# A selective scan rebuilt: broadcasts by DMA, decays in PSUM, products on GpSimd

## The chip, the core and the metric

The kernel runs on one core of a Trainium2 chip. Its time is the device time of one execution in microseconds (us). The engines are named as in the profile: PE is TensorE (matmul), PEld its weight loads, DVE is VectorE, ACT is ScalarE, POOL is GpSimd, SP is SyncE, which here only issues DMAs.

## What is computed

The input is four images of 64 x 64 tokens with 96 channels. Four layers follow each other: a two-dimensional selective scan block, a separable convolution, a linear attention block, and a spectral filter, the last two with a feed-forward block behind them. Only the first layer is changed. Its core, from the reference (b = 4 images, d = 192 channels, n = 16 states, L = 4096 tokens):

```python
def step(h, inp):
    u_t, dt_t, B_t, C_t = inp
    dA = jnp.exp(dt_t[..., None] * A)
    h = dA * h + (dt_t * u_t)[..., None] * B_t[:, None, :]
    y = jnp.sum(h * C_t[:, None, :], axis=-1)
    return (h, y)
...
x_hw = xc.reshape(B, D_INNER, L)
x_wh = jnp.transpose(xc, (0, 1, 3, 2)).reshape(B, D_INNER, L)
x_hwwh = jnp.stack([x_hw, x_wh], axis=0)
xs = jnp.concatenate([x_hwwh, jnp.flip(x_hwwh, axis=3)], axis=0)
...
yy = y[0] + wh_y + inv_y[0] + invwh_y
```

Each image is scanned four times: by rows and by columns, each forwards and backwards. delta, B and C are computed token by token, so the four scans of an image use the same values in different orders. A depends on channel and state. In front of the scan stand a group norm, an input projection, a 3x3 convolution over 192 channels and the projections to delta, B and C; behind it the addition of D u, a gate, an output projection and the residual.

## The kernel before

Arrays stand with channels on the partitions and tokens along them. `layer0` has four parts, written as generators or functions whose pieces a driver strings together. A tile framework inserts the semaphores; it orders the instructions of each engine by the order of the program and by when tiles come free. A tile pool with a tag and a number of buffers (`bufs`) makes the next tile of that tag wait until an older one is released.

`pre(b)` makes everything ahead of the scan, in 8 blocks of 512 tokens: loads (SP), normalisation (ACT), projections and the convolution (PE, `p_conv`), silu and softplus (ACT and DVE). It stores `sz`, `u`, `bc`, `delta` and `du` (delta times u) to DRAM, by DMAs that POOL issues. `post(b)` makes what follows the scan, also in 8 blocks.

The scan works on groups of 8 channels: 8 channels x 16 states fill the 128 partitions, channel by channel. There are 24 groups an image, 96 in all. `decay(b, g)` loads delta of 8 channels (`dl`, 8 rows), lets PE copy each row to 16 partitions (a matmul with the 0/1 matrix `sel`, into `pa`, L248) and ACT write exp(delta A) to `dA` in SBUF (L252), 512 tokens at a time. `scan_group` does the same for du (`pb`, L275); DVE multiplies it with `brep`, B replicated on the partitions, into `dB` (L279). ACT copies both arrays into order by columns (`dAT`, `dBT`, L281). DVE then does the two scans by rows over 4096 tokens (L286, L287), their sum (L290), the two by columns (L294, L295), their sum (L298), the sum of both orders through a transposing view (L299), and the product with `crep`, C replicated (L307). PE sums over the states with the matrix `red` (`py`, L312), ACT copies the sums to `ys` (L315), SP stores them (L317).

In the middle of each group, `beside()` emits pieces of `post` of the image before and of `pre` of the image after, and the next group's `decay`. The first image's `pre` stands alone at the start, the last image's `post` alone at the end of the layer; `layers123` follows.

Of the kernel before, what the change touches and what calls it, by code (L numbers as in the profile page):

```python
# [18 lines left out]
NB = 4  # images  # L19
HW = 64  # rows, and columns, of an image  # L20
L = HW * HW  # tokens of an image
C = 96  # channels
DI = 192  # inner channels of the scan, and hidden ones of the spectral filter
NS = 16  # states of a scanned channel
NG = DI // 8  # groups of 8 scanned channels: 8 channels x 16 states on the partitions
RK = 6
BLK = 512  # tokens of one matmul: 8 image rows
# [3 lines left out]
N1 = 64  # the transform over 4096 tokens is 64 x 64  # L31


def conv_taps():
    """The 3x3 taps (ky, kx), the middle one first: it alone reaches every output."""
    return [(1, 1)] + [(y, x) for y in range(3) for x in range(3) if (y, x) != (1, 1)]


def tap_window(ky, kx, r0):
    """Rows (of the block's, from r0) and columns of the output that a tap reaches."""  # L40
    dy, dx = ky - 1, kx - 1
    ra, rb = max(0, -dy - r0), min(RPB, HW - dy - r0)
    ca, cb = max(0, -dx), min(HW, HW - dx)
    return dy, dx, ra, rb, ca, cb


@with_exitstack
def layer0(ctx: ExitStack, tc: tile.TileContext, a: dict, x1):
    """Group norm, the 2D selective scan block, the residual; x1[b] = relu(x + block), as the
    next layer reads it."""  # L50
# [20 lines left out]
    sel = const("sel", [40, 128], a["sel"])  # L71
# [3 lines left out]
    # Each of the four scans adds D u.  # L75
# [6 lines left out]

    delta_s = dram("delta_s", [DI, L])
    du_s = dram("du_s", [DI, L])
    bc_s = dram("bc_s", [2 * NS, L])
    u_s = dram("u_s", [DI, L])
    sz_s = dram("sz_s", [DI, L])
    y_s = dram("y_s", [DI, L])

    def halves(t):  # L90
        return t.rearrange("(c p) l -> p c l", p=C)
# [3 lines left out]

    def k4(name, shape=(C, 2, BLK)):
        return wk.tile(list(shape), F32, tag="k4", name=name, bufs=4)

    def pre_psum(name, rows=C, cols=BLK):
        t = ps.tile([128, BLK], F32, tag="pre", name=name, bufs=2)  # L100
        return t[:rows, :cols]

    def pre(b):
        """Everything before the scan, in blocks of 8 image rows."""
# [9 lines left out]
        # A group's three channels: its mean, and the mean of variance + squared distance of means.  # L114
# [15 lines left out]
        for i in range(NBLK):  # L130
# [4 lines left out]
            xb = k2("xb", (C, RPB + 2, HW))  # L135
# [3 lines left out]
            xn = k2("xn", (C, RPB + 2, HW))  # L139
            nc.scalar.activation(  # L140
                xn[:, :n, :], xb[:, :n, :], AF.Identity, scale=gn[:, 0:1], bias=gn[:, 1:2]
            )
            xp = k4("xp", (C, 2, RPB + 2, HW))
            for c in range(2):
                for ra, rb in ((0, 5), (5, n)):
                    p = pre_psum("p_xp", C, (rb - ra) * HW)
                    nc.tensor.matmul(
                        p, lhsT=w_in[:, c * C : (c + 1) * C], rhs=xn[:, ra:rb, :],
# [3 lines left out]
            sz = k4("sz")  # L152
            for c in range(2):
# [3 lines left out]
                    rhs=xn[:, r0 - lo : r0 - lo + RPB, :], start=True, stop=True,  # L157
                )
                nc.scalar.activation(sz[:, c, :], p, AF.Silu)  # L159
            nc.gpsimd.dma_start(halves(sz_s[b])[:, :, cols], sz)  # L160
            yield
            u = k4("u")
# [16 lines left out]
            nc.gpsimd.dma_start(halves(u_s[b])[:, :, cols], u)  # L179
# [8 lines left out]
            nc.gpsimd.dma_start(bc_s[b][:, cols], xd[RK : RK + 2 * NS, :])  # L188
            for c in range(2):
# [3 lines left out]
                # softplus(v) = max(v, 0) + log(1 + e), e = exp(-|v|); with w = fl(1 + e), the  # L193
                # logarithm is log(w) - ((w - 1) - e).
# [12 lines left out]
                nc.gpsimd.dma_start(delta_s[b][rows, cols], r)  # L207
                du = k2("du")
                nc.vector.tensor_tensor(du, r, u[:, c, :], ALU.mult)
                nc.gpsimd.dma_start(du_s[b][rows, cols], du)  # L210
            yield

    def post(b):
        """D u, the gate, the output projection and the residual."""
        for i in range(NBLK):
            cols = slice(i * BLK, (i + 1) * BLK)
            y, u, sz = k4("y_in"), k4("u_in"), k4("sz_in")
# [620 lines left out]
```

## Time and profile before

| | us |
|---|---|
| median of two runs | 9806.71 (9795.03 to 9818.39) |
| span of the profiled execution | 9822.7 |
| first scan (L286) starts | 491.7 |
| last copy of sums (L315) ends | 7413.6 |
| DVE busy over the span | 6735.3 (69%) |
| PE busy | 6680.7 (68%) |
| ACT busy | 3202.3 (33%) |
| POOL busy | 159.9 (2%) |

The span is from the first to the last instruction of one execution; the median is over runs of the whole program, and no other time of the profiled execution is given. Between 491.7 and 7413.6 lies the scan stage: 6921.9 us for 96 groups, 72.1 a group. Before it is the first image's `pre`, after it the last `post` and the three later layers. A group of instructions in the profile is one line of the code on one engine; "busy" is the sum of its durations, "mean" that of one. What stands behind the second bar is the time in which its engine was idle just before it, and who ended that idle time.

### The profile page before, as it was taken

The numbers are of one execution on the slowest core, as the hardware profiler recorded it, in microseconds if no ns is written. First come the engines' busy times: TensorE is split into PE (matmuls) and PEld (weight loads), VectorE is DVE, ScalarE is ACT, GpSimd is POOL, SyncE is SP. The second block draws the span as 40 slices with busy tenths as digits, with TensorE's granted clock in tenths as the row PEclk, the third lists the DMA queues.
The fourth block names the chain that finished last, engine by engine and source line by source line (L and its number), as shares of the span: only waits on it lengthen the run. The fifth ranks groups of instructions, "written<-read, shape, count | busy, mean of one in ns | idle before, by whom it ended". The sixth has DMA issues, their size and how long they took to land.

```text
span 9822.7 us, 58304 instructions
## 1 busy us (share of the span) xinstructions
PE 6680.7 (68%) x22202; PEld 3031.3 (31%) x22202; DVE 6735.3 (69%) x3526; ACT 3202.3 (33%) x4081; POOL 159.9 (2%) x296
## 2 busy tenths in 40 slices
PE   6767777754567666555666665554445888989888
PEld 2222222211122222111222211111112766848576
DVE  1188888887888888788988879989993323132232
ACT  3333434342334444333444433333330111121111
POOL 0000000000000000000000000000000000000000
PEclk8855565555566666555656655555556867777776
DMA  1110000002100000210000021000002010100000
GB/s 44 43 25 16 15 13 15 14 20 52 30 15 16 19 17 17 52 39 12 16 18 16 22 44 33 13 6 6 6 5 71 4 36 1 33 7 14 26 1 26
DMA packets 94661, 216.09 MB, mean 22 GB/s; under 512 B 25274, under 2 KB 26958, under 8 KB 92494
## 3 DMA queue, kind: packets, MB, share of 16 engines
q1 hardware_dynamic: 75950, 153.62, 6.4%
q0 software_dynamic: 18432, 58.74, 2.1%
q8 instruction: 177, 2.90, 0.1%
q14 instruction: 102, 0.84, 0.0%
HBM read 134.67 MB, written 77.59 MB: 22 GB/s over the span
## 4 chain that ended last, share of the span: by engine, by line
DVE 42%; PE 39%; ACT 8%; issue 8%; DMA 2%; SPq 0%; POOL 0%; DVEq 0%; ACTq 0%; POOLq 0%
DVE dB L287 8%; DVE T L294 8%; DVE dBT L295 6%; PE pb L275 6%; DVE S L286 6%; PE p_conv L169 5%; DVE S L290 4%; ACT dBT L281 4%; PE pa L248 4%; PE py L312 3%; PE p_l L499 3%; DVE S L299 2%; PE p_dft L653 2%; PE p_h L639 2%; ACT dAT L281 2%
## 5 line engine op out<-in xcount | busy, mean ns | idle before, releaser
L275 PE MATMUL pb<-du_g,sel 8*128 8x512 f32 x1536 | 1309.9, 1022 | 1517.7 <-DVE dB L279 1517.7
L248 PE MATMUL pa<-dl,sel 8*128 8x512 f32 x1536 | 1359.6, 1030 | 879.2 <-ACT dA L252 784.7
L281 ACT COPY dAT<-dA 128x512 f32<-128x512 f32 x768 | 772.3, 1104 | 2020.5 <-DVE dBT L295 2014.5
L286 DVE TENSOR_TENSOR_SCAN S<-dA,dB 128x4096 f32<-128x4096 f32 x96 | 834.4, 8692 | 576.2 <-PE py L312 494.2
L169 PE MATMUL p_conv<-xp,conv_w 96*96 96x504 f32 (+3 forms) x2304 | 1204.7, 684 | 2.8 <-ACT sz L159 2.8
L275 PEld LDWEIGHTS pb<-du_g,sel 8*128 8x128 f32 x1536 | 447.7, 307 | 2317.7 <-DVE dB L279 1843.4
L248 PEld LDWEIGHTS pa<-dl,sel 8*128 8x128 f32 x1536 | 411.2, 296 | 1762.8 <-ACT dA L252 1082.3
L287 DVE TENSOR_TENSOR_SCAN dB<-dA,dB 128x4096 f32<-128x4096 f32 x96 | 833.9, 8686 | 5.6 <-DVE S L286 0.5
L294 DVE TENSOR_TENSOR_SCAN T<-dAT,dBT 128x4096 f32<-128x4096 f32 x96 | 833.4, 8681 | 0.0
L295 DVE TENSOR_TENSOR_SCAN dBT<-dAT,dBT 128x4096 f32<-128x4096 f32 x96 | 833.2, 8679 | 0.1
L281 ACT COPY dBT<-dB 128x512 f32<-128x512 f32 x768 | 771.8, 1094 | 130.9 <-DVE T L298 80.8
L252 ACT ACTIVATE dA<-pa,nega 128x512 f32<-128x512 f32 x768 | 513.8, 685 | 715.2 <-PE pa L248 671.4
L299 DVE TENSOR_TENSOR S<-S,T 128x4096 f32<-128x4096 f32 x96 | 716.2, 7460 | 1.1
L169 PEld LDWEIGHTS p_conv<-xp,conv_w 96*96 96x96 f32 x2304 | 423.0, 190 | 802.8 <-issue 779.2
L279 DVE TENSOR_TENSOR dB<-pb,brep 128x512 f32<-128x512 f32 x768 | 492.9, 679 | 251.5 <-PE pb L275 201.8
L312 PE MATMUL py<-S,red 128*32 128x512 f32 x1536 | 401.7, 955 | 201.2 <-DVE S L307 177.3
L307 DVE TENSOR_TENSOR S<-S,crep 128x1024 f32<-128x1024 f32 x384 | 445.8, 1220 | 1.9
L290 DVE TENSOR_TENSOR S<-S,dB 128x4096 f32<-128x4096 f32 x96 | 424.4, 4421 | 2.0
L298 DVE TENSOR_TENSOR T<-T,dBT 128x4096 f32<-128x4096 f32 x96 | 423.9, 4416 | 0.3
L201 DVE TENSOR_SCALAR w<-e 96x512 f32<-96x512 f32 x64 | 26.3, 411 | 391.1 <-ACT e L199 391.1
L499 PE MATMUL p_l<-x,taps 96*96 96x504 f32 (+3 forms) x576 | 249.8, 597 | 29.8 <-DMA x<-x 29.8
L376 DVE COPY o<-p_o 128x192 f32<-128x192 f32 x64 | 22.9, 357 | 318.4 <-ACT o L372 318.4
(183 smaller groups left out, 6638.2 us busy)
## 6 DMA issues: line engine op xcount, KB each, us to landing
tw<-in_dft SPq DMA_DIRECT2D x32, 512.0 KB
sz_s<-sz POOLq DMA_DIRECT2D x32, 384.0 KB, 3.4
u_s<-u POOLq DMA_DIRECT2D x32, 384.0 KB, 3.4
delta_s<-r POOLq DMA_DIRECT2D x64, 192.0 KB, 2.4
du_s<-du POOLq DMA_DIRECT2D x64, 192.0 KB, 2.4
dl<-delta_s SPq DMA_DIRECT2D x384, 32.0 KB
du_g<-du_s SPq DMA_DIRECT2D x384, 32.0 KB
y_s<-ys SPq DMA_DIRECT2D x768, 16.0 KB
```

Source lines behind the costliest of these rows:

```text
L169: nc.tensor.matmul(p[:, ra:rb, ca:cb], lhsT=conv_w[:, kc, ky * 3 + kx, oc * C : (oc + 1) * C], rhs=xp[:, kc, at + ra : at + rb, ca + dx : ...
L248: nc.tensor.matmul(pa, lhsT=sel[0:8, :], rhs=dl[:, (q % 2) * BLK : (q % 2 + 1) * BLK], start=True, stop=True,)
L275: nc.tensor.matmul(pb, lhsT=sel[32:40, :], rhs=du[32:40, (q % 2) * BLK : (q % 2 + 1) * BLK], start=True, stop=True,)
L281: nc.scalar.copy(dst.rearrange("p (w h) -> p w h", h=HW)[:, :, hs], src[:, cols].rearrange("p (h w) -> p w h", w=HW),)
L286: nc.vector.tensor_tensor_scan(S, dA, dB, 0.0, ALU.mult, ALU.add)
L287: nc.vector.tensor_tensor_scan(dB[:, ::-1], dA[:, ::-1], dB[:, ::-1], 0.0, ALU.mult, ALU.add)
L290: nc.vector.tensor_tensor(S, S, dB, ALU.add)
L294: nc.vector.tensor_tensor_scan(T, dAT, dBT, 0.0, ALU.mult, ALU.add)
L295: nc.vector.tensor_tensor_scan(dBT[:, ::-1], dAT[:, ::-1], dBT[:, ::-1], 0.0, ALU.mult, ALU.add)
L299: nc.vector.tensor_tensor(S.rearrange("p (h w) -> p h w", w=HW), S.rearrange("p (h w) -> p h w", w=HW), T.rearrange(by_col, h=HW), ALU.add,)
L312: nc.tensor.matmul(py[k : k + 32, :], lhsT=red, rhs=S[:, cols], start=True, stop=True)
L499: nc.tensor.matmul(p3[:, ra:rb, ca:cb], lhsT=taps[:, ky * 3 + kx, :], rhs=x3[:, r0 + dy + ra : r0 + dy + rb, ca + dx : cb + dx], start=(k ...
```

## The change

The scan now runs in phases: (image, group, order), 192 of them, with order 0 by rows and 1 by columns. The layout on the partitions is state by state (16 states x 8 channels). The tokens go in steps of `CH` = 1024, four a phase.

- `load` fetches delta and du of 8 channels by DMA straight to 128 partitions, each row of 4 KB read 16 times: 8 DMAs of 512 KB a phase. The matrix `sel` and its matmuls are gone.
- `inputs`: POOL multiplies du with the replicated B in place, for the next phase.
- `decay`: ACT writes exp(delta A) of 1024 tokens to PSUM (two buffers of two banks), once for the forward scan and once more for the backward one.
- `scan`: DVE does four forward scans of 1024, each started from the last column of the one before, and four backward ones in place. POOL adds the two directions and multiplies with the replicated C. PE, ACT and SP then sum, copy and store as before, for each order by itself.
- `turn`: transposes an array of up to 96 rows: load 4096 tokens a row, four copies on ACT through a transposing view, four stores. `pre` calls it for bc and for each half of delta and du, `post` for each half of the sums by columns. This replaces the copies of L281 and the add of L299.
- `replicas`: four DMAs of 2 MB an image replace the 16 of 256 KB. `beside()` calls it in the last phase of an image.
- Every DMA that POOL issued in `layer0` is now issued by SP. Buffers of `pre` and `post` change: `xp` has one, `u` two, `xn` is gone (in place), and `post` works by halves of the channels.
- `beside()` spreads the pieces of `post` and `pre` over the first 42 of an image's 48 phases.

The matrix `red` and the layout of `a_logs` follow the new order of the partitions. The diff, without `pre`'s and the later layers' small edits:

```diff
+CH = 1024
+NCH = L // CH
...
+    delta_s = [dram("delta_s", [DI, L]), dram("deltaT_s", [DI, L])]
+    du_s = [dram("du_s", [DI, L]), dram("duT_s", [DI, L])]
+    bc_s = [dram("bc_s", [2 * NS, L]), dram("bcT_s", [2 * NS, L])]
+    y_s = [dram("y_s", [DI, L]), dram("yT_s", [DI, L])]
+    y2_s = dram("y2_s", [DI, L])
...
+    def turn(src, dst):
+        n = src.shape[0]
+        t = wk.tile([C, L], F32, tag="turn", name="turn")
+        nc.sync.dma_start(t[:n, :], src)
+        for q in range(NCH):
+            o = wk.tile([C, CH], F32, tag="turned", name="turned")
+            w = CH // HW
+            nc.scalar.copy(
+                o[:n, :].rearrange("p (w h) -> p w h", h=HW),
+                t[:n, :].rearrange("p (h w) -> p w h", w=HW)[:, q * w : (q + 1) * w, :],
+            )
+            nc.sync.dma_start(dst[:, q * CH : (q + 1) * CH], o[:n, :])
...
     def pre(b):
...
+        turn(bc_s[0][b], bc_s[1][b])
+        yield
+        for c in range(2):
+            rows = slice(c * C, (c + 1) * C)
+            turn(delta_s[0][b][rows, :], delta_s[1][b][rows, :])
+            yield
+            turn(du_s[0][b][rows, :], du_s[1][b][rows, :])
+            yield
     def post(b):
+        for c in range(2):
+            rows = slice(c * C, (c + 1) * C)
+            turn(y_s[1][b][rows, :], y2_s[b][rows, :])
+            yield
...
+            for c in range(2):
+                rows = slice(c * C, (c + 1) * C)
+                y, y2, u = k2("y_in"), k2("y2_in"), k2("u_in")
+                nc.sync.dma_start(y, y_s[0][b][rows, cols])
+                nc.sync.dma_start(y2, y2_s[b][rows, cols])
+                nc.sync.dma_start(u, u_s[b][rows, cols])
+                nc.vector.scalar_tensor_tensor(y, u, d4[:, c : c + 1], y, ALU.mult, ALU.add)
+                sz = k2("sz_in")
+                nc.sync.dma_start(sz, sz_s[b][rows, cols])
+                nc.vector.tensor_tensor(y, y, y2, ALU.add)
+                nc.vector.tensor_tensor(y, y, sz, ALU.mult)
+                nc.tensor.matmul(p, lhsT=w_out[:, c, :], rhs=y, start=(c == 0), stop=(c == 1))
...
-    def decay(b, g):
...
-    def scan_group(b, g, dA, brep, crep, beside):
...
+    def load(b, g, o):
+        rows = slice(g * 8, (g + 1) * 8)
+        dl, du = [], []
+        for q in range(NCH):
+            for dst, src, n, tag, bufs in ((dl, delta_s, "dl", "dl", 5), (du, du_s, "B", "B", 6)):
+                t = big.tile([128, CH], F32, tag=tag, name=n, bufs=bufs)
+                nc.sync.dma_start(
+                    t, src[o][b][rows, chunk(q)].unsqueeze(0).broadcast_to([NS, 8, CH])
+                )
+                dst.append(t)
+        return dl, du
+    def inputs(b, g, o, du):
+        for q in range(NCH):
+            nc.gpsimd.tensor_tensor(du[q], du[q], reps[o, 0][:, chunk(q)], ALU.mult)
+    def decay(g, dl, q):
+        pa = ps.tile([128, CH], F32, tag="pa", name="pa", bufs=2)
+        nc.scalar.activation(pa, dl[q], AF.Exp, scale=nega[:, g : g + 1])
+        return pa
+    def scan(b, g, o, dl, B, beside):
+        rows = slice(g * 8, (g + 1) * 8)
+        S = []
+        for q in range(NCH):
+            pa = decay(g, dl, q)
+            s = big.tile([128, CH], F32, tag="S", name="S", bufs=6)
+            nc.vector.tensor_tensor_scan(
+                s, pa, B[q], S[-1][:, CH - 1 : CH] if S else 0.0, ALU.mult, ALU.add
+            )
+            S.append(s)
+        beside()
+        last = None
+        for q in reversed(range(NCH)):
+            pa = decay(g, dl, q)
+            nc.vector.tensor_tensor_scan(
+                B[q][:, ::-1], pa[:, ::-1], B[q][:, ::-1],
+                last[:, 0:1] if last is not None else 0.0, ALU.mult, ALU.add,
+            )
+            last = B[q]
+            nc.gpsimd.tensor_tensor(S[q], S[q], B[q], ALU.add)
+            nc.gpsimd.tensor_tensor(S[q], S[q], reps[o, 1][:, chunk(q)], ALU.mult)
+            if q % 2 == 1:
+                py = ps.tile([128, BLK], F32, tag="py", name="py")
+            for k in range(2):
+                at = 32 * (2 * (q % 2) + k)
+                nc.tensor.matmul(
+                    py[at : at + 32, :], lhsT=red, rhs=S[q][:, k * BLK : (k + 1) * BLK],
+                    start=True, stop=True,
+                )
+            if q % 2 == 0:
+                ys = wk.tile([128, BLK], F32, tag="ys", name="ys", bufs=2)
+                nc.scalar.copy(ys, py)
+                for j in range(4):
+                    i = 2 * q + j
+                    nc.sync.dma_start(
+                        y_s[o][b][rows, i * BLK : (i + 1) * BLK], ys[32 * j : 32 * j + 8, :]
+                    )
+    reps = {}
+    def replicas(b):
+        for o in range(2):
+            for k in range(2):
+                t = big.tile([128, L], F32, tag=f"rep{o}{k}", name=f"rep{o}{k}")
+                nc.sync.dma_start(
+                    t, bc_s[o][b][k * NS : (k + 1) * NS, :].unsqueeze(1).broadcast_to([NS, 8, L])
+                )
+                reps[o, k] = t
     for _ in pre(0):
         pass
+    phases = [(b, g, o) for b in range(NB) for g in range(NG) for o in range(2)]
+    replicas(0)
+    loaded = load(*phases[0])
+    inputs(*phases[0], loaded[1])
+    for n, (b, g, o) in enumerate(phases):
+        here = n % (2 * NG)
+        if here == 0:
+            aside = chain(post(b - 1) if b > 0 else (), pre(b + 1) if b + 1 < NB else ())
+            n_aside = (NBLK + 2 if b > 0 else 0) + (3 * NBLK + 6 if b + 1 < NB else 0)
+            done = 0
+        nxt = phases[n + 1] if n + 1 < len(phases) else None
+        ahead = []
+        def beside():
+            nonlocal done
+            if nxt is not None:
+                if nxt[0] != b:
+                    replicas(nxt[0])
+                ahead.append(load(*nxt))
+                inputs(*nxt, ahead[0][1])
+            while done < min(n_aside, n_aside * (here + 1) // (2 * NG - 6)):
+                next(aside)
+                done += 1
+        scan(b, g, o, *loaded, beside)
+        if ahead:
+            loaded = ahead[0]
```

## The prediction

> **What bounds the kernel now.** I read the windows first (where is the time), then the costliest groups, then the chain of waits, then the DMA part. Lines, engines and tiles are those of the kernel before.
>
> The windows give the scan stage by itself, from the first scan (491.7) to the last copy of sums (7413.6). Columns: length, then busy time (instructions) of PE, PEld, DVE, ACT, POOL, then clock, DMA share, GB/s:
>
> ```profile
> 491.70:7413.60 6921.90, 4243.39 (x6892) 1325.99 (x6890) 6002.20 (x2203) 2643.22 (x3130) 106.21 (x192) 0.57 0.08 20
> ```
>
> 70% of the span is this stage. DVE is busy 6002 of 6922 us, POOL 106, DMA at 8%. The groups say with what; the figure after the bar is the sum, then the mean in ns:
>
> ```profile
> L286 DVE TENSOR_TENSOR_SCAN S<-dA,dB 128x4096 f32<-128x4096 f32 x96 | 834.4, 8692 | 576.2 <-PE py L312 494.2
> ...
> L299 DVE TENSOR_TENSOR S<-S,T 128x4096 f32<-128x4096 f32 x96 | 716.2, 7460 | 1.1
> ...
> L279 DVE TENSOR_TENSOR dB<-pb,brep 128x512 f32<-128x512 f32 x768 | 492.9, 679 | 251.5 <-PE pb L275 201.8
> ...
> L307 DVE TENSOR_TENSOR S<-S,crep 128x1024 f32<-128x1024 f32 x384 | 445.8, 1220 | 1.9
> L290 DVE TENSOR_TENSOR S<-S,dB 128x4096 f32<-128x4096 f32 x96 | 424.4, 4421 | 2.0
> ```
>
> Per group of 8 channels (96 of them) DVE does four scans (8.69 each, 34.7), the transposing add 7.46, two plain adds 8.8, the B products 5.1, the C products 4.6: 60.8 us of a stage step of 6921.9/96 = 72.1. The rest are waits at both ends of a group (py, pb). The chain of waits agrees:
>
> ```profile
> DVE 42%; PE 39%; ACT 8%; issue 8%; DMA 2%; SPq 0%; POOL 0%; DVEq 0%; ACTq 0%; POOLq 0%
> ```
>
> So a group is DVE's 60.8 us plus about 11 of hand-over. The new loop runs 192 phases (a group in one order of the image); per phase the old stage costs 36.05 us.
>
> **What DVE loses.** All but the scans leave it. A scan of 4096 takes 8.69, a plain product 1.220 at 1024 and 4.421 at 4096: slope 1.042 ns an element, 0.15 fixed. A scan is so 2.08 ns an element plus 0.15: 2.29 for 1024 tokens. A phase has eight, 18.3 us; with the work of `pre` and `post` under 21. DVE ceases to be the bound.
>
> **What POOL gets.** Twelve products or sums of 128x1024 a phase: 4 with B, 4 sums of directions, 4 with C. No such row exists: POOL's only work on data is
>
> ```profile
> L627 POOL MEMSET ln_s<- 1x4096 f32 x4 | 14.0, 3507 | 53.5 <-PE p_att L588 53.5
> L556 POOL MEMSET lt<- 128x4 f32 x32 | 3.3, 106 | 1814.5 <-PE p_gram L559 1776.7 <-DVE s L475 32.9 <-PE p_tok L554 4.9
> ```
>
> 0.856 ns an element for one written stream, 0.10 fixed. A product has three streams. All overlapped: 0.98 us for 1024; one after another: 2.73; two of three overlapped: 1.85. I take the middle of the last two, 2.29 (an estimate): the memset is the only POOL row, and I see no reason that all its streams run at once. 12 x 2.29 = 27.5 us a phase, more than DVE's 18.3: POOL becomes the bound.
>
> The Trainium skill speaks against this move ("GPSIMD Engine Reference", section "Performance versus the Vector engine"): elementwise work with two inputs is about twice as slow there, 4497 ns for 2048 fp32 elements. By that price an operation would be 2.25 and the total about 90 us lower; no run here shows it yet.
>
> **What POOL and DVE take from each other.** They hardly ever worked together in this trace, so ends only: nothing, or full exclusion (rival C). I put down only DVE's instructions that, like POOL's, read two SBUF operands: four of `pre` per half block, three of `post`, 64 and 48 an image, three images of each in the stage, 336 x 0.68 (row L206) = 228 us, 1.2 a phase. The scans now read one operand from PSUM.
>
> A rule of the skill bears on this ("SBUF — State Buffer", section "Who interferes with whom"): a DVE instruction with at most one SBUF input does not contend with GpSimd, one with two does and blocks for a whole instruction. It would make the exclusion of rival C nil; no trace here tests it.
>
> **DMA.** Eight loads of 512 KB a phase replace two 32 KB loads in each pair of blocks: 4.19 MB. To it come, per image, with 3.1 MB for 192 channels: `pre` reads x twice (3.4) and writes four arrays and bc (13.1), the seven turns read and write delta, du, y and bc (19.9), `post` reads four arrays and x and writes x1 (15.7), the replicas take 8.4. That is 60.5 MB, 1.3 a phase, and with 0.13 for the sums 5.6 MB a phase in all. The nearest shape is the `tw` load, also 512 KB in 128 rows of 4 KB; a window with one of them alone and one with all engines full at the head of the later layers, and then two windows of the replica loads before the first scan:
>
> ```profile
> 7504.00:7508.00 4.00, 0.00 (x0) 0.00 (x0) 3.65 (x13) 0.56 (x2) 0.00 (x0) 0.50 1.04 250
> ...
> 7840.00:7844.00 4.00, 3.52 (x28) 2.61 (x24) 0.68 (x1) 0.60 (x1) 0.00 (x0) 1.00 0.42 131
> ```
>
> ```profile
> 472.00:476.00 4.00, 0.00 (x0) 0.00 (x0) 0.00 (x0) 0.75 (x1) 0.00 (x0) 0.50 1.13 131
> 476.00:480.00 4.00, 0.00 (x0) 0.00 (x0) 0.00 (x0) 0.00 (x0) 0.00 (x0) 0.50 0.90 118
> ```
>
> 131/0.42 = 312 GB/s for `tw`; 118/0.90 to 131/1.13, about 120 GB/s, where eight loads each fill 16 partitions from one source. The new loads have the `tw` target (128 partitions, 4 KB rows) but a source read 16 times. I take the 250 of the full window: 5.6 MB are 22 us a phase, under POOL's 27.5; the 120 is rival B. A turn's load of 1.5 MB goes ahead of the phase's loads, 6.3 us at 250; the 21 turns that fall into the stage are 132 us, 0.7 a phase, which I charge in full because only two spare B tiles are there to cover.
>
> **Waits added, and what stands behind them.** SP: the load of a B tile waits for POOL's sum that frees it (6 tiles, 4 in use); behind it stand the stores of sums and all transfers of `pre` and `post`, which leave POOL's queue (0.52 to 0.67 us each there) for SP's. A phase has 8 loads, 8 stores and about 4 others: 20 x 0.35 (SP's dl and y_in rows: 0.26 to 0.44) = 7 us, hidden under 27. ACT: an exponential waits for a PSUM tile that a scan frees; behind it the copies of sums and `pre`. Eight of 0.685 + 512 x 0.844 ns (slope from the xp copies, 422 at 320 and 368 at 256) = 1.12 are 8.9 us, with sums, turns and `pre` about 15: hidden. If a convolution holds ACT (up to 30 us in the waits of `u`), DVE has 9 us a phase to give before POOL starves. PE loses the 2669 us of L275 and L248 and stays hidden. POOL: a sum waits for the reverse scan; behind it the next phase's products. Were these last in its queue, two scans (4.6 us) a phase would be bare; since the first two of the next phase's B tiles are free, I cost that at nothing (rival D is its price).
>
> **Start, image borders, end.** A turn is its load 7, then four times a transposing copy (2.0, from L281's 1.10 for 512) and a store of 384 KB (3.4 to landing) through one buffer: 29 us. Three must be done before the first phase by columns, less the phase before it: 60; `pre` has fewer buffers (one xp for four): 5 us for each of 8 blocks, 40. Start 100. At three image borders 8.4 MB of replicas precede the loads: 8.4/0.25 = 34 us each, 101. (The C products of an image's last phase read the next image's replicas as the code stands, so they wait for them too.) Two turns before the last `post`: 58.
>
> **The sum.** Phase: 27.5 + 1.2 + 0.7 = 29.4, times 192 = 5645. Outside the stage 9822.7 - 6921.9 = 2900.8 unchanged; start, borders and end 100 + 101 + 58 = 259. 2900.8 + 5645 + 259 = 8805 for the span of a profiled execution. The one shown is 9822.7, 16 above the median of the runs, 9806.7 (what lies around the span is not given); so 8789, rounded 8790. Break-even is a phase of (6921.9 - 259)/192 = 34.7 us, that is 2.73 us for a POOL operation.
>
> **Rivals.**
> A, POOL overlaps its streams: then DMA or DVE sets 23 us a phase, 2900.8 + 4416 + 259 = 7580. For it: the memset's one element in 0.856 ns; against: three streams.
> B, the loads are the bound: at 120 GB/s 5.6 MB take 46.7 us, 8966 for the stage, about 12130. It decides below 5.6/34.7 = 161 GB/s. For it: the 120 GB/s of the replica loads, which share a source; against: those fill 16 partitions at a time, and `tw` runs at 312.
> C, DVE's scans and POOL exclude each other: 27.5 + 18.3 + 0.7 = 46.5, 8928 for the stage, about 12090, slower. It decides from the point where 6.5 of the 18.3 us are lost. For it: both would read SBUF all the time; against: one operand of the scan lies in PSUM.
> D, the order of POOL's queue leaves two scans bare, or the three streams run one after another: 34.0 or 34.7 a phase, 9690 or 9820: no change.
>
> **Chances.** Forecast, 8300 to 9500: 0.60. A 0.06, B 0.14, C 0.11, D 0.09. Faster by over 2% (about what a measurement of this kernel can tell from no change) is the forecast and A, 0.66; within 2% D, 0.09; slower B and C, 0.25. The range runs from 8300 to 10500: out of it lie A, half of B (milder rates stay within) and most of C, about 0.2. The forecast's own range is 8300 to 9500.
>
> **What would show it.** Right: POOL's 2304 operations of 128x1024 at 2.1 to 2.5 us, POOL busy over 85% of the stage, the 1536 scans at 2.29, DVE busy 65 to 70%, the chain of waits on POOL lines, DMA share 0.5 to 0.8. Wrong: scans far above 2.3 or POOL above 2.7 (C), POOL waiting mostly for DMA with a share near 1 (B), POOL waiting for DVE after each phase (D).

## The result, and the profile after

| | before | after |
|---|---|---|
| median, us | 9806.71 | 10247.22 (10240.87 to 10253.57) |
| after / before | | 1.0445 (95% interval 1.0407 to 1.0483) |
| span of the profiled execution | 9822.7 | 10239.0 |
| first scan starts | 491.7 | 401.2 |
| scan stage | 6921.9 | 7397.3 |
| a phase, stage / 192 | 36.05 | 38.5 |
| span outside the stage | 2900.8 | 2841.7 |

The change makes the kernel 4.5% slower. All of the loss lies in the scan stage, from the first scan (L297) to the last copy of sums (L323); what lies around it became 59 us shorter. The window of the stage, with the columns of the window shown before:

```profile
401.20:7798.50 7397.30, 2633.09 (x5388) 557.78 (x5388) 4124.02 (x1995) 2668.64 (x2729) 5438.66 (x2303) 0.57 0.57 139
```

DVE fell from 6002 to 4124 us, 56% of the stage. POOL rose from 106 to 5439, but that is only 74% of the stage: no engine is full, and the DMA share is 0.57. A stage that is longer than the work of its fullest engine by 1959 us waits for something. The costliest groups say who waits (sum and mean of one, then the idle time in front of them and who ended it):

```profile
L310 POOL TENSOR_TENSOR S<-S,B 128x1024 f32<-128x1024 f32 x768 | 1851.3, 2418 | 1255.2 <-DVE B L305 1241.4 <-PE p_dt L207 13.1
L283 POOL TENSOR_TENSOR B<-B,rep 128x1024 f32<-128x1024 f32 x768 | 1792.2, 2356 | 995.5 <-DMA rep<-bc_s 398.4 <-DMA B<-duT_s 345.8 <-DMA B<-du_s 251.3
L311 POOL TENSOR_TENSOR S<-S,rep 128x1024 f32<-128x1024 f32 x768 | 1834.9, 2397 | 103.6 <-DMA rep<-bcT_s 70.7
L305 DVE TENSOR_TENSOR_SCAN B<-pa,B 128x1024 f32<-128x1024 f32 x768 | 1791.3, 2332 | 89.5 <-ACT pa L287 27.0 <-DVE B L305 0.5
L297 DVE TENSOR_TENSOR_SCAN S<-pa,S,B 128x1024 f32<-128x1024 f32 x576 | 1353.0, 2349 | 762.5 <-POOL B L283 601.3 <-PE py L317 79.4 <-ACT pa L287 42.7
```

POOL's three groups are 5478 us of work. The sum L310 waited 1241 us for the backward scan, 6.5 a phase. Of the 995.5 in front of L283, 398 lie before the stage; its next two releasers are the loads of B, 345.8 (`duT_s`) and 251.3 (`du_s`): 597 us, 3.1 a phase. With 71 for a replica and 13 for a matmul: 5478 + 1241 + 597 + 84 = 7400, about the whole stage (records that follow each other overlap by hundredths of a us). So POOL is the engine to follow, and the two waits, 1838 us, are nearly all that the stage takes beyond POOL's own work.

The chain of waits no longer answers the question; followed back from the last instruction it breaks off in the later layers, and its shares add up to a fifth of the span:

```profile
PE 19%; DVE 2%; ACT 1%; DMA 0%; issue 0%; SPq 0%; ACTq 0%; DVEq 0%; POOL 0%
```

The timeline shows a phase with nothing of `pre` or `post` beside it (start, length, engine, line, tiles, count; in brackets the idle time before and who ended it). POOL:

```profile
6473.51 2.36 POOL L310 TENSOR_TENSOR S<-S,B 128x1024 f32<-128x1024 f32 x1
6475.82 2.35 POOL L283 TENSOR_TENSOR B<-B,rep 128x1024 f32<-128x1024 f32 x1
6478.11 2.35 POOL L311 TENSOR_TENSOR S<-S,rep 128x1024 f32<-128x1024 f32 x1
6480.41 6.96 POOL L283 TENSOR_TENSOR B<-B,rep 128x1024 f32<-128x1024 f32 x3
6492.68 2.34 POOL L310 TENSOR_TENSOR S<-S,B 128x1024 f32<-128x1024 f32 x1 [5.31 <-DVE B L305]
...
6506.60 2.36 POOL L310 TENSOR_TENSOR S<-S,B 128x1024 f32<-128x1024 f32 x1
```

The last sum of one phase, then all four products with B of the next (call it X), and then POOL stands for 5.31 us. From 6473.51 to 6506.60 the phase takes 33.1 us: 12 operations of 2.3 and the gap. In the gap DVE does the last forward and the first backward scan of X:

```profile
6482.80 7.32 DVE L297 TENSOR_TENSOR_SCAN S<-pa,S,B 128x1024 f32<-128x1024 f32 x3 [2.31 <-POOL B L283]
6490.22 9.65 DVE L305 TENSOR_TENSOR_SCAN B<-pa,B 128x1024 f32<-128x1024 f32 x4
```

And SP's queue, in the same stretch:

```profile
6466.69 0.52 SPq L274 DMA_DIRECT2D B<-duT_s  x1
6473.90 11.18 SPq L326 DMA_DIRECT2D y_s<-ys  x8
6485.13 0.52 SPq L274 DMA_DIRECT2D dl<-delta_s  x1
6485.77 0.52 SPq L274 DMA_DIRECT2D B<-du_s  x1
```

The load at 6466.69 is X's last. The loads for the phase after X stand behind the eight stores of sums of the phase before X. These take 11.2 us, because the last four wait for that phase's last sums to pass POOL (until 6480.5), PE (6482.4) and ACT (6483.1). Only at 6485 does a load go out, although two B tiles have been free, one since 6469 and one since 6476, when the last sums that read them ended.

Stretches with `turn`, `pre` or `post` beside are worse. SP's and POOL's timelines in such a stretch:

```profile
6416.94 1.82 SPq L326 DMA_DIRECT2D y_s<-ys  x4
6427.41 0.31 SPq L117 DMA_DIRECT2D y_s<-turned  x1
6427.76 0.52 SPq L274 DMA_DIRECT2D dl<-delta_s  x1
```

```profile
6435.83 2.34 POOL L283 TENSOR_TENSOR B<-B,rep 128x1024 f32<-128x1024 f32 x1 [5.89 <-DMA B<-du_s]
6443.55 2.34 POOL L283 TENSOR_TENSOR B<-B,rep 128x1024 f32<-128x1024 f32 x1 [5.38 <-DMA B<-du_s]
```

A store of a turned array waits for ACT's copy; the queue behind it, loads included, stands still until 6427, and POOL waits 5.9 and 5.4 us for the loads. SP's own waits, over the span (total, times, longest):

```profile
SPq L326 <- ACT ys L323: 1418.6, 245, 22.2
SPq L117 <- ACT turned L113: 912.7, 109, 25.8
```

These two are 2331 us in which SP waits for something to store and can't issue a load.

### The profile page after: what moved, and what is told of

It is laid out like the page before. It is cut to its first block, busy times and chain, and to the rows that moved or that the text cites. A ratio compares the mean times of both kernels' runs of the same rounds, so it can differ in the third digit from the quotient of the medians.

```text
span 10239.0 us, 62095 instructions
## 1 busy us (share of the span) xinstructions
PE 5039.0 (49%) x20666; PEld 2239.5 (22%) x20666; DVE 4865.2 (48%) x3334; ACT 3220.1 (31%) x3664; POOL 5458.6 (53%) x2344
## 5 line engine op out<-in xcount | busy, mean ns | idle before, releaser
L317 PE MATMUL py<-S,red 128*32 128x512 f32 x3072 | 1397.9, 995 | 4422.2 <-POOL S L311 4339.5
L310 POOL TENSOR_TENSOR S<-S,B 128x1024 f32<-128x1024 f32 x768 | 1851.3, 2418 | 1255.2 <-DVE B L305 1241.4
L283 POOL TENSOR_TENSOR B<-B,rep 128x1024 f32<-128x1024 f32 x768 | 1792.2, 2356 | 995.5 <-DMA rep<-bc_s 398.4
L287 ACT ACTIVATE pa<-dl,nega 128x1024 f32<-128x1024 f32 x1536 | 1712.6, 1118 | 1870.3 <-DVE S L297 881.9
L311 POOL TENSOR_TENSOR S<-S,rep 128x1024 f32<-128x1024 f32 x768 | 1834.9, 2397 | 103.6 <-DMA rep<-bcT_s 70.7
L305 DVE TENSOR_TENSOR_SCAN B<-pa,B 128x1024 f32<-128x1024 f32 x768 | 1791.3, 2332 | 89.5 <-ACT pa L287 27.0
L297 DVE TENSOR_TENSOR_SCAN S<-pa,S,B 128x1024 f32<-128x1024 f32 x576 | 1353.0, 2349 | 762.5 <-POOL B L283 601.3
L297 DVE TENSOR_TENSOR_SCAN S<-pa,B 128x1024 f32<-128x1024 f32 x192 | 439.6, 2290 | 2296.4 <-POOL B L283 2092.0
L323 ACT COPY ys<-py 128x512 f32<-128x512 f32 x384 | 224.9, 586 | 2616.6 <-PE py L317 2575.2
L677 PE MATMUL p_dft<-dft,hb 128*64 128x64 f32 x3072 | 227.2, 317 | 9.4 <-DVE hb L667 9.4
L677 PEld LDWEIGHTS p_dft<-dft,hb 128*64 128x64 f32 x3072 | 225.5, 251 | 11.2 <-DVE hb L667 11.2
L663 PE MATMUL p_h<-w1s,ln_s 97*64 97x64 f32 x3072 | 225.6, 314 | 3.5 <-DVE ln_s L562 3.5
```

What stands on the lines that cost most here:

```text
L283: nc.gpsimd.tensor_tensor(du[q], du[q], reps[o, 0][:, chunk(q)], ALU.mult)
L287: nc.scalar.activation(pa, dl[q], AF.Exp, scale=nega[:, g : g + 1])
L297: nc.vector.tensor_tensor_scan(s, pa, B[q], S[-1][:, CH - 1 : CH] if S else 0.0, ALU.mult, ALU.add)
L305: nc.vector.tensor_tensor_scan(B[q][:, ::-1], pa[:, ::-1], B[q][:, ::-1], last[:, 0:1] if last is not None else 0.0, ALU.mult, ALU.add,)
L310: nc.gpsimd.tensor_tensor(S[q], S[q], B[q], ALU.add)
L311: nc.gpsimd.tensor_tensor(S[q], S[q], reps[o, 1][:, chunk(q)], ALU.mult)
```

## The experiments

The theory drawn from this profile: SP's queue, which works in order, holds the next phase's loads behind stores that wait for late results. The rivals: too few spare tiles of delta; DVE and POOL excluding each other (rival C); the order of POOL's own queue alone (rival D); the work of `pre` and `post` as such. Ratios are to the kernel before, with 95% intervals.

### Stores on ACT's queue

```diff
-            nc.sync.dma_start(dst[:, q * CH : (q + 1) * CH], o[:n, :])
+            nc.scalar.dma_start(dst[:, q * CH : (q + 1) * CH], o[:n, :])
...
-                    nc.sync.dma_start(
+                    nc.scalar.dma_start(
                         y_s[o][b][rows, i * BLK : (i + 1) * BLK], ys[32 * j : 32 * j + 8, :]
```

and the same for the stores of `sz`, `u`, `bc` and `x1`. The stores of delta and du, which DVE makes, stay on SP.

> The changed kernel with one edit: stores whose data ACT makes (ys, the turned arrays, sz, u, bc, x1) are issued by ACT behind their copy and no longer by SP; so SP's queue holds the loads and the two stores of DVE results. In the changed kernel POOL's stage of 7397 us is 5478 us of work, 1241 us of waits for the backward scan and 597 us of waits for B loads. Theory 1 (SP's one queue: a load stands behind stores that wait for the end of a phase, so the next phase's B tiles come late and POOL's products for it are queued behind this phase's sums): both waits all but vanish, stage 29 to 31 us a phase, total 8450 to 8850 us. Theory 2 (the broadcast loads are simply slow, DMA-bound): nothing moves, 10100 to 10300. Theory 3 (POOL and DVE exclude each other beyond the two-input instructions): nothing moves either, and POOL's operations stay above 2.35 us.

Measured: 9245.23 us, 0.9428 (0.9413 to 0.9444). The change is now a gain of 5.7%, with no edit but the queue of some stores. POOL's wait for the loads falls from 597 to 112 us, for the backward scan from 1241 to 785. POOL's groups in a window in which nothing of `pre` or `post` lies beside:

```profile
L310 POOL TENSOR_TENSOR S<-S,B 128x1024 f32<-128x1024 f32 x40 | 93.4, 2346 | 3.4 <-DVE B L305 3.4
L311 POOL TENSOR_TENSOR S<-S,rep 128x1024 f32<-128x1024 f32 x40 | 93.3, 2345 | 1.6
L283 POOL TENSOR_TENSOR B<-B,rep 128x1024 f32<-128x1024 f32 x40 | 93.0, 2350 | 0.0
```

Ten phases in the 280 us from 6500 to 6780, 28.0 each, and POOL idle for 5 us: the phase whose work on POOL the prediction had put at 27.5. The changed kernel did 31 sums in the same window, there with a few pieces of `post` beside. The direction was expected; the total is 395 us above the top of my range. The waits that remain, in POOL's wait and in DVE's forward scans:

```profile
POOL S L310 <- DVE B L305: 785.0, 199, 17.1
L297 DVE TENSOR_TENSOR_SCAN S<-pa,S,B 128x1024 f32<-128x1024 f32 x576 | 1353.0, 2349 | 1893.2 <-ACT pa L287 1237.9 <-POOL B L283 624.4 <-ACT ys L323 4.5
```

They lie where `pre` and `post` are beside: of the 785 us, 3.4 fall into the window above.

Then the two parts alone, the stores of sums first:

> Half of the edit of e1: only the stores of the sums (ys, eight a phase) leave SP's queue for ACT's; the stores of pre, post and the turns stay with SP. Theory 1: the sums' stores wait for the end of a phase and are what makes the next phase's B loads late, so most of the gain of e1 comes from here: total 9350 to 9750 us, POOL's wait for the backward scan falls from 1241 to 700 to 900 us, its wait for B loads (597) stays above 300. Rival (the transfers of pre and post in SP's queue are the larger part): 9850 to 10200.

Measured: 9304.40, 0.9483 (0.9465 to 0.95), a little better than expected. POOL's wait for the backward scan is 788 us, as expected; the one for the loads fell to 166, where I had expected it to stay above 300.

> The other half of the edit of e1: the stores of sz, u, bc, x1 and of the turned arrays go to ACT's queue, the stores of the sums stay with SP. Theory 1: POOL's wait for B loads falls from 597 to under 250 us, its wait for the backward scan stays at 1100 to 1300, total 9750 to 10050. Rival (as before): 9300 to 9600.

Measured: 9889.10, 1.0083 (1.0065 to 1.0101); the total is as expected. POOL's waits:

```profile
POOL S L310 <- DVE B L305: 1388.1, 212, 14.8
POOL B L283 <- DMA B<-du_s: 71.2, 15, 43.3
POOL B L283 <- DMA B<-duT_s: 30.6, 11, 9.9
```

The stores of sums are worth 943 us, the others 358, both 1002: each alone uncovers part of the same time. With the sums still on SP, POOL's wait for loads falls to 102 us, but the one for the backward scan rises to 1388, above the 1100 to 1300 that I had expected.

### The order of the loads

```diff
-        for q in range(NCH):
-            for dst, src, n, tag, bufs in ((dl, delta_s, "dl", "dl", 5), (du, du_s, "B", "B", 6)):
+        for k, q in ((1, 0), (1, 1), (0, 0), (0, 1), (1, 2), (0, 2), (1, 3), (0, 3)):
```

> The changed kernel with one edit: a phase's loads are issued B0, B1, delta0, delta1, B2, delta2, B3, delta3 instead of delta0, B0, delta1, B1 and so on. Theory 1a (the one spare delta tile is what holds B back, since the second B load stands behind a delta load that waits for the backward exponential): the first two products of the next phase fit into the gap, the 5 us a phase that POOL waits for the backward scan go, total 9200 to 9500 us. Theory 1b (the stores in the same queue hold the loads back, whatever their order): within 1.5% of the changed kernel, 10100 to 10400.

Measured: 10401.14, 1.062 (1.0599 to 1.0641), with 566 us of waits for B loads against 597. It is 1.5% slower than the changed kernel, at the edge of the range for theory 1b; POOL's wait for the backward scan grew from 1241 to 1425. The loads of B are no earlier when they stand ahead of those of delta, so that delta has one spare tile and B two is not the cause.

### Without the work beside

All four `pre` stand ahead of the phases, all four `post` behind them.

> The changed kernel with the work of pre for all four images ahead of the scan stage and post for all four behind it, so that the stage holds scans alone (its own loads and stores of sums stay). What is read is the length of the stage, not the total, which grows by the three pre and post that are no longer beside it (to some 10500 to 10800 us). Theory 1: the steady phase of the changed kernel, 33.1 us (twelve operations of 2.35 and a gap of 5 us in which POOL waits for the last forward and the first backward scan), holds throughout: 192 x 33.2 = 6370 us against 7397; the rest of the loss, 5.3 us a phase, was the transfers of pre and post in SP's queue. Theory 2 (bandwidth): the stage stays above 36 us a phase.

Measured: 10213.22, 1.0417 (1.0397 to 1.0438). The stage is 7009 us, not the 6370 that I had expected: the scheduler still mixed some of the later images' `pre` into the phases up to 2000 us, so total and stage say little. The window 6000 to 7000 is free of it:

```profile
L310 POOL TENSOR_TENSOR S<-S,B 128x1024 f32<-128x1024 f32 x123 | 287.3, 2346 | 164.7 <-DVE B L305 164.7
L311 POOL TENSOR_TENSOR S<-S,rep 128x1024 f32<-128x1024 f32 x121 | 282.2, 2343 | 2.4
L283 POOL TENSOR_TENSOR B<-B,rep 128x1024 f32<-128x1024 f32 x120 | 278.5, 2341 | 0.0
```

121 of each in 1000 us are phases of 33.1. No load is late in this window, and still each phase has its 5.3 us. So there are two losses: a steady one, the gap of every phase, and one that comes with the work beside.

The same with the stores on ACT:

> All stores of layer0 on ACT's queue, and pre and post of all images taken out of the phases: four pre before them, four post behind them. Theory (SP's queue is the whole cause of the 5.3 us that POOL stands bare in each phase, and what is left of the waits with the stores on ACT comes from pre and post beside the phases): a phase free of them goes from the 33.1 us seen without asides to POOL's own 28.0 to 28.6, and POOL's wait for the backward scan, 785 us with the stores on ACT, falls under 150 outside the first 2000 us. Total 9250 to 9450, since pre and post now stand alone. Rival (the copy of sums in ACT, or the order of the scans, keeps part of the wait with no work beside): phases of 30 us or more, waits for the backward scan of 2 us a phase, total 9600 and above.

Measured: 9247.63, 0.9431 (0.9405 to 0.9457). POOL's timeline:

```profile
3398.24 6.95 POOL L283 TENSOR_TENSOR B<-B,rep 128x1024 f32<-128x1024 f32 x3
3405.53 2.34 POOL L310 TENSOR_TENSOR S<-S,B 128x1024 f32<-128x1024 f32 x1 [0.35 <-DVE B L305]
...
3426.49 6.95 POOL L283 TENSOR_TENSOR B<-B,rep 128x1024 f32<-128x1024 f32 x3
```

28.25 us a phase, and the gap is 0.35. The total is 2 us under the theory's range; my bound for the wait outside the first 2000 us (150) was missed, 263. Gathering the work brought nothing against 9245: it costs as much ahead of the stage, behind it and beside the first 32 phases as it did spread over the stage.

This timeline also differs from the changed kernel's in POOL's order: of the three products at 3398.24 two belong to the next phase. Counted over POOL's instructions, in 181 of the changed kernel's 192 phases none of the next phase's products stands ahead of a phase's first sum. With the stores on ACT two of them stand there in 183 phases; with the sums' stores alone moved in 142, with the others alone in 9. Moving stores had changed POOL's order too; I take it that the framework places instructions by when it expects their inputs. Two causes lay in one experiment.

### The order on POOL, and the loads, taken apart

First the changed kernel, stores on SP, with two of the next phase's products set ahead of the first sum by hand, as they stand with the stores on ACT:

```diff
+            made.append(nc.gpsimd.tensor_tensor(du[q], du[q], reps[o, 0][:, chunk(q)], ALU.mult))
...
+            if len(made) > 1:
+                m = made[1][1]
+                with tc.issue_after(m.ins if hasattr(m, "ins") else m):
+                    nc.gpsimd.tensor_tensor(S[q], S[q], B[q], ALU.add)
```

> The changed kernel with its stores left on SP's queue; only POOL's queue is ordered by hand: the first two products of the next phase stand ahead of the first sum of this one, as they do in most phases of the kernel with its stores on ACT, and as they seldom do in the changed kernel. Theory (the loads are the cause: the next phase's loads stand in SP's queue behind the stores of the phase before, and these wait for the last sums; products placed early find no data): POOL trades its 5.3 us wait for the backward scan for a wait of 4 to 8 us for the loads of B in each phase, and the time stays at 10000 to 10700. Rival (only POOL's order matters, the data are there in time): phases fall to POOL's own 28.3 us where nothing lies beside them, B loads cost under 2 us a phase, total 9200 to 9600.

Measured: 10552.73, 1.076 (1.0736 to 1.0784). The group of the products (L284 here):

```profile
L284 POOL TENSOR_TENSOR B<-B,rep 128x1024 f32<-128x1024 f32 x768 | 1804.5, 2357 | 2691.7 <-DMA B<-du_s 1170.2 <-DMA B<-duT_s 1116.4 <-DMA rep<-bc_s 395.6
```

The wait for the backward scan is gone (45 us), and 2287 us of waits for loads stand in its place, 11.9 a phase, more than the 4 to 8 that I had expected. With the stores on SP the data are not there when the good order asks for them.

Second the reverse: stores on ACT, and all products of the next phase behind the last sum.

```diff
-                inputs(*nxt, ahead[0][1])
...
+            m = nc.gpsimd.tensor_tensor(S[q], S[q], B[q], ALU.add)
...
+            with tc.issue_after(m):
+                inputs(*nxt, loaded[1])
```

> All stores on ACT's queue, as in the run with 9245, and POOL's queue ordered by hand as it is in most phases of the changed kernel: all four products of the next phase behind the last sum of this one. Theory (with data in time, this order alone leaves DVE's last forward and first backward scan bare): the 5.3 us wait for the backward scan is back in each phase, 33.1 us where nothing lies beside, wait for the backward scan 1000 to 1300 us in all, total 9900 to 10200. Rival (the loads alone are the cause, the order on POOL is a by-product): phases of 28 to 29 us, total 9200 to 9400.

Measured: 9645.25, 0.9829 (0.9811 to 0.9847). The gap is back exactly, 33.3 us from one phase to the next:

```profile
6503.34 2.34 POOL L310 TENSOR_TENSOR S<-S,B 128x1024 f32<-128x1024 f32 x1 [5.32 <-DVE B L305]
...
6536.66 2.35 POOL L310 TENSOR_TENSOR S<-S,B 128x1024 f32<-128x1024 f32 x1 [5.32 <-DVE B L305]
```

The waits are as expected, the total is 255 us below my range: I had forgotten that the loads' own waits stay away in this kernel. Side by side:

| | us | POOL waits for the backward scan | for loads of B |
|---|---|---|---|
| stores on ACT | 9245 | 785 | 112 |
| stores on ACT, products behind | 9645 | 1239 | 86 |
| changed kernel | 10247 | 1241 | 597 |
| changed kernel, products ahead | 10553 | 45 | 2287 |

From the first row to the second only POOL's order is edited: 400 us, with 454 more of waits for the backward scan and 65 less of waits for loads and replicas (the framework then places some of DVE's and ACT's instructions differently too). From the second to the third the order is mostly the same and the stores move to SP: 602 us, of which the waits for loads explain 511 and those for replicas 71. The fourth says that the order can't be mended alone. Both parts come with the stores in SP's queue, one at run time, the other through the order that the framework then chose. That it chose it for this reason is argued from the kernels that differ in the stores' queue alone; I haven't seen its estimates.

### Do DVE and POOL exclude each other?

The backward scan's decay goes to SBUF (in place of delta) rather than PSUM:

```diff
-            pa = decay(g, dl, q)
+            pa = dl[q]
+            nc.scalar.activation(pa, dl[q], AF.Exp, scale=nega[:, g : g + 1])
```

> The changed kernel with one edit: in the backward half the exponential is written over the delta tile in SBUF, not to PSUM, so that a backward scan reads two operands from SBUF and a forward scan still one. If two SBUF operands make DVE and POOL exclude each other (in the changed kernel the two-input products of pre take 0.68 us at the least and up to 2.84, and POOL operations 2.33 at the least and up to 3.5), backward scans lengthen from 2.33 to 3.5 to 4.7 us in the mean while forward ones stay at 2.33, POOL's operations lengthen too, and the total rises to 10700 to 11800. If it doesn't matter where the operand lies, scans and total stay as they are, within 1.5% of 10247.

Measured: 11240.80, 1.1466 (1.1443 to 1.1488). Groups of POOL (the sum is L311 here) and of DVE:

```profile
L311 POOL TENSOR_TENSOR S<-S,B 128x1024 f32<-128x1024 f32 x768 | 2615.4, 3413 | 1138.8 <-DVE B L306 1138.8
```

```profile
L306 DVE TENSOR_TENSOR_SCAN B<-dl,B 128x1024 f32<-128x1024 f32 x768 | 2373.6, 3091 | 43.4 <-ACT dl L305 7.6 <-DVE S L297 1.4
```

The backward scan goes from 2.33 to 3.09 us, the sum beside it from 2.42 to 3.41; the forward scans, still with PSUM, stay at 2.35. The mean hides two kinds: 454 of the 768 backward scans took under 2.5 us and 302 over 4, longer by most of a POOL operation. The exclusion is there, for two SBUF operands, and was not what made the changed kernel slow. I had expected 3.5 to 4.7 us for these scans; the total lies in the range for this case.

### Was the copy of sums in ACT's way?

With the stores on ACT, the copy and stores of a phase's last sums were put behind the second exponential of the next phase.

> e1 with one edit more: the copy of a phase's last sums and its four stores stand in ACT's queue behind the next phase's second exponential instead of ahead of it. In e1 DVE's forward scans wait 1238 us for exponentials and POOL 785 us for backward scans; the theory is that ACT's queue waits for POOL's last product and holds the next exponentials back. Then POOL's wait falls under 500 us and the total to 8850 to 9100. Rival (what holds ACT is pre and post: convolutions, turns and their stores): 9150 to 9300.

Measured: 9222.71, 0.940 (0.938 to 0.9419), 0.24% below the kernel without this edit and in the rival's range; the wait for the backward scan is 772 us against 785. The copy is not what is left. That `pre` and `post` hold ACT, as the rival has it, is not shown by this.

### Less work for POOL

With the stores on ACT, the backward scan writes over its decay in PSUM, and DVE instead of POOL adds the directions.

```diff
-                B[q][:, ::-1], pa[:, ::-1], B[q][:, ::-1],
+                pa[:, ::-1], pa[:, ::-1], B[q][:, ::-1],
...
-            nc.gpsimd.tensor_tensor(S[q], S[q], B[q], ALU.add)
+            last = pa
+            nc.vector.tensor_tensor(S[q], S[q], pa, ALU.add)
```

> e1 with one edit more: the backward scan writes over its decay in PSUM, and DVE, not POOL, adds it to the forward state (one operand in SBUF, one in PSUM). POOL is left with eight products a phase (18.9 us), DVE gets 4 x 1.22 more (18.6 + 4.9 = 23.5, with pre and post about 25.5). If POOL's twelve operations bound e1, a phase goes from 33 to 26 to 29 us, total 7950 to 8550. The adds should take 1.2 to 1.3 us, not more, since only one of their operands is in SBUF. Rival (ACT's queue or the loads bound e1: 5.6 MB a phase at 250 GB/s are 22.4 us): 8700 to 9250.

Measured: 8972.05, 0.9147 (0.9132 to 0.9162): better than with POOL's sum, but above my range and in the rival's (ACT's queue or the loads set the pace). In a quiet window (5600 to 5800) POOL does 28 products with B, seven phases of 28.6 us, where DVE has 23 us of work. DVE's first scans wait for ACT:

```profile
L297 DVE TENSOR_TENSOR_SCAN S<-pa,S,B 128x1024 f32<-128x1024 f32 x576 | 1353.2, 2349 | 707.2 <-ACT pa L287 639.5 <-POOL B L283 17.7 <-DVE S L297 1.0
```

The decay tile is now held by the backward scan and by the sum behind it, and there are two. So a third one, for which `pre` gives up two of its three PSUM buffers:

> Stores on ACT, backward scan in place in PSUM and DVE's sum, as in the run with 8972, with three PSUM buffers for the decays in place of two; pre has one PSUM buffer in place of three to make room. Theory (the decay tile is held by the backward scan and its sum, so DVE waits 6.0 us a phase for the next exponential; DVE's own work is 23.2 us of a 28.6 us phase free of pre and post): phases of 23.3 to 24.5 us where nothing lies beside them, DVE's wait for ACT under 1 us, DMA share near 0.7, total 8000 to 8450 if pre on one buffer costs little. Rival 1 (the loads or the pre work set the pace, not the decay tiles): phases of 27 us or more, total 8850 and above. Rival 2 (the tiles are the cause, but a pre on one PSUM buffer gives it back): phases of 24 where nothing lies beside, longer ones beside pre, total 8500 to 9000.

Measured: 8796.07, 0.8963 (0.894 to 0.8986). In the same window POOL does 34 products with B, 23.5 us a phase, and DVE, busy for 191 of the 200 us, waits 6 for ACT: there the tiles were the cause. From 3000 to 4000, with `pre` and `post` beside, it is 128 products, 31 us a phase, against 125 with two tiles: there the third tile gains next to nothing, and what sets the pace is not shown. The first scan starts at 524 us against 400, since the first `pre` now has one PSUM buffer. The total is in the range of rival 2. This is the fastest version, 10.4% below the kernel before. That it lands on the predicted figure is chance; it is another kernel.

## Why the prediction was wrong, point by point

The forecast was 8790 us for the change as it stands, and it measured 10247. That lies inside the wide range of 8300 to 10500 by luck: the range was wide for milder forms of B and C, and neither happened. The forecast's own range ended at 9500, and the kernel became slower. Its sum had 5645 for the phases and 161 for turns and borders in the stage, 5806, where the stage takes 7397: 1591 too little. Outside the stage it had 2999 (40 for the first `pre`, 58 at the end), measured 2842.

- POOL's work: 27.5 + 1.2 a phase, 5510 us; its rows add up to 5478. An operation was estimated at 2.29 and took 2.35 (median); the other price given there, 2.25, was 4% low. The estimate was the middle of two bounds with no row for a product behind it, and its 0.856 ns an element still held the memset's fixed part (0.83 without, which would give 2.23), so that it came this close is partly luck. The lengthening by DVE's two-operand instructions is real (quiet phases 2.34, the means of the stage 2.36 to 2.42), but about 0.5 a phase and not 1.2: two small errors cancel.
- DVE: scans 2.29 predicted, 2.29 to 2.35 measured. ACT: 1.12 and 1.118. Both right.
- DMA: 250 GB/s assumed; 139 GB/s at a share of 0.57 are 244 at full load. Rival B is out: with the same loads and the stores on ACT POOL's wait for them falls from 597 to 112 us, so they were late because they were issued late, not because they were slow.
- Rival C is out: with one operand in PSUM the scans keep their time beside POOL. Here the Trainium skill ("SBUF — State Buffer", section "Who interferes with whom") agrees with the chip on both sides, the lossless scans and, with two SBUF inputs, the rise of the mean from 2.33 to 3.09 us.
- Start: the first scan came 90 us earlier, and what the turns cost showed as a late load: before the first phase by columns POOL stood 52 us for `duT_s`. The end cost 52 us (from the last copy of sums to the first matmul of the next layer 147 against 95), predicted 58.
- **The step that failed, first half:** "A phase has 8 loads, 8 stores and about 4 others: 20 x 0.35 ... = 7 us, hidden under 27". I counted SP's queue by the time that it takes to issue. What counts in a queue is what stands behind an entry that waits: SP stood 1419 us for copies of sums and 913 for turned arrays, with loads behind. The working had listed the stores behind the loads' wait; it never asked what stands behind the stores' wait. The late loads, put at 0.7 us a phase, are 3.1. The profile of the kernel before had the sign, a queue that stood for copies of sums, once for longer than a phase:

```profile
SPq L317 <- ACT ys L315: 1521.6, 187, 51.8
```

- **The second half:** "since the first two of the next phase's B tiles are free, I cost that at nothing". The tiles are free, but their loads are not issued, and the products take their place behind the sums: 5.3 us bare in a quiet phase (rival D had 4.6), 6.5 on the mean.
- A term that is wrong besides: "ACT ... hidden", with 9 us a phase for DVE to give. With the stores on ACT the stage is 6426 us, still 620 above the sum's 5806 (outside it 2829, 170 below 2999). POOL stands 785 us there for the backward scan, and DVE's forward scans stand 1238 us for ACT's exponentials, where `pre` and `post` lie beside. That the second wait causes the first is argued, and what holds the exponentials stays open; it is not the copy of sums.
- Rival D had the place right and the price of its own part nearly: phases of 34.0 predicted for two bare scans, 33.3 measured from one phase to the next with the bad order and the loads in time. That its total of 9690 is so near the 9645 of that run is chance, since the run has waits that D did not count. D stopped there. That the same queue would also hold the loads, another 600 us, was in no rival; "no change" at 0.09 was the nearest that I came to a loss from a queue.
- The signs that I gave: POOL over 85% busy and DVE 65 to 70% would have shown the forecast right; they are 74% and 56%. "POOL waiting for DVE after each phase" would have shown D, and does. The forecast's phase exists: 28.0 to 28.3 us, once the stores leave SP.

## What to carry to other kernels

When DMAs are moved to another queue, don't multiply their number by the time of an issue: write the queue down in its order and ask of each entry what it waits for and which load stands behind it. A store waits for the end of a chain, a prefetch for nothing; in one queue the store makes the prefetch as late as itself, and the spare buffers are worth nothing. Where a framework orders the engines, a late load also changes the order of the compute instructions, so compare these orders before you explain a gap by either.

## What the hardware showed that I had not expected

- The choice of the issuing queue alone is worth 1002 us here (10247 to 9245), 10%, some 400 of them through the order on POOL that the framework chose. The Trainium skill ("DMA: Bandwidth & Descriptors", section "Issuing engines are not separate DMA queues") says that several issuing engines save only the time of initiating. No run here speaks against that for the transfers, and all runs of the changed kernel and its variants move the same 984 MB read and 130 MB written; but the time of the kernel goes by the waits in the queue.
- The loads that read each source row 16 times ran in a stage with 139 GB/s at a share of 0.57, or 244 at full share, near the 250 of the full window with `tw` loads before the change and twice the 120 or so of the replica loads there. No run reads the rows once, so what the repetition costs is not shown.
- Exclusion shows as a longer instruction, not as idle time: row L220 of the changed kernel, 96x512, has 0.66 us at least and 2.84 at most (L206, the row of that shape before the change, 0.67 to 0.71), and an operation on 96x1 elements took up to 2.27:

```profile
L134 DVE TENSOR_TENSOR gn<-mv,gn x4: 155/1212/2269, 21.0 to 4724.3; 96x1 f32<-96x1 f32 x4
```

(minimum, median and maximum in ns). In the runs with DVE's sum an add with one operand in PSUM took 1.22 beside a busy POOL, as the plain product of 1024 did before the change.
